# First norms in a row, the first additions of bv put off, an adjacency stage placed under the arrival of Wq, and separate output buffers for the last two batches

## The chip, the cores and the metric

The kernel runs on one core of one Trainium2 chip. The metric is device time in microseconds (us), from start to end of one execution. A profile was taken of one execution of each kernel; its span, from the first to the last instruction, is about 2 us shorter than the device time of the same execution. Where I give a moment without more words, it is counted from the start of that span.

Engine names as in the profile: PE is TensorE (matrix products), PEld its weight loads, DVE is VectorE, ACT is ScalarE, POOL is GpSimd, SP is SyncE. A "q" behind a name is a DMA issue from that engine's queue.

## The reference, cut to what matters

128 batches, each with 128 nodes and 512 features, all float32. Two layers share one adjacency matrix `adj` (128 x 128):

```python
# layer 0
h = maximum(layernorm(x), 0)
A = einsum('od,bdn->bon', adj, h);  C = A + b
x = x + max over j of relu(A[j] + (C - A)[i])      # = relu(max_n A + b): one number c per node
# layer 1: 8 heads of 64
h = maximum(layernorm(x), 0)
q, k, v = h @ Wq + bq, h @ Wk + bk, h @ Wv + bv
w = softmax(q k^T / 8 + (-1e9 where adj == 0))
x = x + w v
```

The second layer norm sees x + c, and c is constant along the features, so it cancels there. The kernel therefore computes h once for each batch, uses it for the adjacency product (whose maximum gives c) and, transposed, for Q, K and V. It adds x, c, bv and the attention's result at the end.

## The kernel before: the parts that the change and the argument touch

Four batches form a group. The first group's Q is computed plainly, everything later with a seven-product scheme. The norm and its end, with the addition of the bias bv on GpSimd:

```python
def norm(m):
    ...
    nc.vector.bn_stats(st, X[g][:, i, :]); nc.vector.bn_aggr(mv, st)
    nc.vector.tensor_scalar_add(ve, mv[:, 1:2], EPS)
    nc.gpsimd.tensor_tensor(rstd, ve, mhalf, op=ALU.pow)          # GpSimd
def norm_end(m):
    nc.vector.tensor_scalar(HN[m], X[g][:, i, :], MV[m][:, 0:1], 0.0, op0=ALU.subtract, op1=ALU.max)
    nc.scalar.activation(HN[m], HN[m], AF.Copy, scale=RSTD[m])
    nc.gpsimd.tensor_tensor(X[g][:, i, :], X[g][:, i, :], bv_sb, op=ALU.add)   # GpSimd, needs bv
def transposes(m):      # 4 PE transposes into one PSUM tile, ACT copies it to HT
def adjacency(m, pa):   # 1 product into PSUM (two matmul records), DVE takes the maximum
```

The beginning (`early(m)` is `transposes(m)` and then `adjacency(m)`), and the first group's K and V:

```python
for m in range(G):                    # G = 4
    norm(m); norm_end(m)
    if m > 0: early(m - 1)
plain_q(0)                            # bias copies on ACT after each half of a PSUM bank
early(G - 1)
weight_sums(nc.vector, "k"); ...h_sum(0, k)...
plain_q(1)
weight_sums(nc.gpsimd, "v")
for s, p in enumerate((k.p1, k.p6, k.p2, ..., v.p4)):   # 13 products
    p()
    m = G + s // 2
    if s % 2 == 0: norm(m); norm_end(m)      # one product ahead of its use
    elif m < 2 * G: early(m)
    else: blocks(m); adjacency(m, ...)
```

The end. `finish` forms w v, divides by the sums, adds x and c, and sends the batch out:

```python
def finish(g, i, w, spare=False, eng=nc.vector):
    ...                                                   # 32 matmuls, reciprocal on DVE
    o = work.tile([P, 2, 4, HD], F32, name="o")           # a pool of two buffers
    nc.vector.tensor_tensor(o, po[...], rs..., op=ALU.mult)
    if eng is nc.vector: eng.scalar_tensor_tensor(y, x_b, c_b, y, op0=ALU.add, op1=ALU.add)
    else: nc.scalar.activation(x_b, x_b, AF.Identity, bias=c_b); eng.tensor_tensor(y, x_b, y, op=ALU.add)
    nc.sync.dma_start(out[b], y)
...
w3 = scores(g, 3, spare=True)
finish(g, 0, w0, eng=nc.gpsimd)
PR[g][2].p3()                                             # V's last product and its addition on DVE
masks(w3)                                                 # two DVE multiplications
finish(g, 1, w1, eng=nc.gpsimd)
finish(g, 2, w2, spare=True, eng=nc.gpsimd)
finish(g, 3, w3)
```

## Time and profile before

The time before is 1616.66 us, the median of four runs (1614.24 to 1617.54); three of them were known when the prediction was made. The profiled span is 1614.1 us. I cut it at five moments. PE's busy time is from the view by windows, at these bounds to 0.1 us.

| Stage of before | from | to | length | PE busy |
|---|---|---|---|---|
| start, until Wq's first product | 0 | 19.80 | 19.80 | 7.54 |
| Q of the first group, until the first K product | 19.80 | 38.32 | 18.52 | 16.24 |
| K and V of the first group, until the first scores | 38.32 | 74.72 | 36.40 | 30.72 |
| main loop, until the last score product | 74.72 | 1598.32 | 1523.60 | 1523.60 |
| end, until the last output sum is done | 1598.32 | 1610.30 | 11.98 | 7.49 |

To read it: in the main loop PE is busy without a gap, so nothing that happens on another engine there matters. In the four other stages PE stands for 12.3, 2.3, 5.7 and 4.5 us. These are the only places where the order of work can win time, some 25 us, and part of that is unavoidable (the first loads, the last output).

### The profile page before, as it was taken

Reading aid. Unit: us, or ns where it says so; the run is one execution under the profiler, and the core shown is the slowest. Engines: PE = TensorE matmul, PEld = TensorE weight load, DVE = VectorE, ACT = ScalarE, POOL = GpSimd, SP = SyncE. Lnnn points to the kernel's source line nnn. Section 1 sums busy time; section 2 is a strip of 40 time slices with the busy share of each in tenths; the row PEclk is TensorE's granted clock in tenths of the full one; section 3 lists DMA queues with packets and bytes.
Section 4 is the critical chain, followed back from the end, with each engine's and each line's share of the span. In section 5 each row is a group of like instructions: output and inputs, shape, how many; then the busy total and the mean of one; then the engine's idle time right before and its main releaser. Section 6 shows DMA issues by size and latency. Waiting matters only on the chain.

```text
span 1614.1 us, 29483 instructions
## 1 busy us (share of the span) xinstructions
PE 1585.8 (98%) x11821; PEld 1318.7 (82%) x11821; DVE 1111.7 (69%) x2044; ACT 425.0 (26%) x847; POOL 263.7 (16%) x281
## 2 busy tenths in 40 slices
PE   6899999999999999999999999999999999999997
PEld 4688888888888888888888888888888888888886
DVE  3576777767777767777667777676776677676655
ACT  2322222222222222222222222222222222222222
POOL 4311111111111111111111111111111111111100
PEclk9999999999999999999999999999999999999999
DMA  4033222232222322222322222322122222223111
GB/s 165 1 73 72 68 56 55 66 79 68 65 45 69 71 73 68 60 50 72 72 69 63 47 69 70 79 63 69 43 70 72 71 68 50 60 69 79 41 30 45
DMA packets 299082, 104.02 MB, mean 64 GB/s; under 512 B 264448, under 2 KB 264576, under 8 KB 298944
## 3 DMA queue, kind: packets, MB, share of 16 engines
q1 hardware_dynamic: 297520, 99.69, 24.5%
q8 instruction: 94, 1.54, 0.4%
q10 hardware_dynamic: 1248, 2.16, 0.4%
q14 instruction: 44, 0.36, 0.1%
q0 software_dynamic: 176, 0.27, 0.1%
HBM read 37.03 MB, written 33.55 MB: 44 GB/s over the span
## 4 chain that ended last, share of the span: by engine, by line
PE 97%; DVE 1%; ACT 1%; POOL 0%; issue 0%; DMA 0%; ACTq 0%; DVEq 0%; POOLq 0%
PE mm L373 72%; PE sc L483 9%; PE pav L511 8%; PE mm L307 6%; PE mm L446 1%; PE pav L307 1%; PE sc L300 0%; POOL rstd L265 0%; DMA xg<-in_x_dram 0%; ACT hn L273 0%; POOL xg L274 0%; DVE st L260 0%; DMA out_dram<-o 0%; ACT qT L451 0%; DVE o L520 0%
## 5 line engine op out<-in xcount | busy, mean ns | idle before, releaser
L265 POOL TENSOR_TENSOR rstd<-ve,mhalf 128x1 f32<-128x1 f32 x128 | 84.5, 660 | 1225.6 <-DVE ve L263 978.5
L494 ACT ACTIVATE w<-sc 128x512 f32<-128x512 f32 x252 | 136.8, 594 | 504.6 <-PE sc L483 504.6
L511 PEld LDWEIGHTS pav<-v,w 128*64 128x64 f32 x4032 | 127.9, 137 | 91.9 <-issue 47.8
L373 PE MATMUL mm<-hs,sq_sb 128*128 128x256 f32 x744 | 179.0, 383 | 0.0
L373 PE MATMUL mm<-sv_sb,hs 128*128 128x256 f32 x768 | 176.6, 379 | 0.0
L373 PE MATMUL mm<-hs,sk_sb 128*128 128x256 f32 x768 | 176.4, 379 | 0.0
L274 POOL TENSOR_TENSOR xg<-xg,bv_sb 128x512 f32<-128x512 f32 x128 | 163.2, 1275 | 34.9 <-DVE hn L270 27.4
L499 DVE TENSOR_TENSOR w<-w,live 128x512 f32<-128x512 f32 x252 | 162.1, 684 | 2.0 <-ACT w L494 2.0
L273 ACT ACTIVATE hn<-hn,rstd 128x512 f32<-128x512 f32 x128 | 92.8, 725 | 267.4 <-DVE hn L270 206.2
L373 PEld LDWEIGHTS mm<-sv_sb,hs 128*128 128x128 f32 x768 | 145.8, 190 | 20.8 <-issue 1.0
L373 PEld LDWEIGHTS mm<-hs,sk_sb 128*128 128x128 f32 x768 | 145.9, 190 | 20.3 <-issue 0.5
L373 PEld LDWEIGHTS mm<-hs,sq_sb 128*128 128x128 f32 x744 | 138.8, 190 | 21.4
L483 PE MATMUL sc<-qT,kT 64*128 64x128 f32 x2048 | 148.7, 285 | 0.0
L511 PE MATMUL pav<-v,w 128*64 128x65 f32 x4032 | 145.3, 224 | 0.0
L483 PEld LDWEIGHTS sc<-qT,kT 64*128 64x128 f32 x2048 | 124.2, 187 | 10.1 <-issue 1.7
L421 DVE TENSOR_TENSOR u<-mm,p1b 128x512 f32<-128x512 f32 x63 | 43.5, 691 | 128.0 <-PE mm L373 128.0
L373 PE MATMUL mm<-hT,wk_sb 128*128 128x256 f32 x512 | 124.2, 385 | 0.0
L373 PE MATMUL mm<-wv_sb,hT 128*128 128x256 f32 x512 | 121.1, 379 | 0.0
L307 PE MATMUL mm<-hn,adjT 128*128 128x512 f32 x236 | 120.5, 592 | 0.0
L373 PE MATMUL mm<-hT,wq_sb 128*128 128x256 f32 x496 | 120.4, 386 | 0.0
L373 PEld LDWEIGHTS mm<-wv_sb,hT 128*128 128x128 f32 x512 | 97.2, 190 | 13.7 <-issue 0.5
L373 PEld LDWEIGHTS mm<-hT,wk_sb 128*128 128x128 f32 x512 | 94.7, 190 | 15.8 <-issue 0.5
(97 smaller groups left out, 2045.5 us busy)
## 6 DMA issues: line engine op xcount, KB each, us to landing
out_dram<-o SPq DMA_DIRECT2D x128, 256.0 KB, 2.1
xg<-in_x_dram SPq DMA_DIRECT2D x62, 512.0 KB, 5.2
hT<-tb SPq DMA_DIRECT2D x960, 32.0 KB, 1.9
xg<-in_x_dram SPq DMA_DIRECT2D x2, 256.0 KB, 3.3
xg<-in_x_dram ACTq DMA_DIRECT2D x2, 256.0 KB, 5.6
wq_sb<-in_L_gnn_Wq_dram SPq DMA_DIRECT2D x1, 512.0 KB, 7.9
wk_sb<-in_L_gnn_Wk_dram SPq DMA_DIRECT2D x1, 512.0 KB, 11.0
wq_sb<-in_L_gnn_Wq_dram ACTq DMA_DIRECT2D x1, 512.0 KB, 11.2
```

What stands on the lines that cost most here:

```text
L265: nc.gpsimd.tensor_tensor(rstd, ve, mhalf, op=ALU.pow)
L273: nc.scalar.activation(HN[m], HN[m], AF.Copy, scale=RSTD[m])
L274: nc.gpsimd.tensor_tensor(X[g][:, i, :], X[g][:, i, :], bv_sb, op=ALU.add)
L307: nc.tensor.matmul(pa, adjT, HN[m], start=True, stop=True)
L373: nc.tensor.matmul(bank[:, r, :], lhs, rhs, start=first and r == 0 and c == 0, stop=r == 1 and c == 1, skip_group_check=True,)
L421: nc.vector.tensor_tensor(self.u3, self.b, self.pf[1], op=ALU.add)
L446: nc.tensor.matmul(bank[:, r, :], W["q"][:, c, k * P : (k + 1) * P], h[:, :, c], start=r == 0 and c == 0, stop=r == 1 and c == NC - 1, ski ...
L483: nc.tensor.matmul(psc[:, j, f, :], KT[g][r, f, i * D : (i + 1) * D], QT[g][r, f, i * D : (i + 1) * D], start=True, stop=True,)
L494: nc.scalar.activation(w[:, j], psc[:, j], AF.Exp, scale=HD ** -0.5)
L499: nc.vector.tensor_tensor(w[:, j], w[:, j], live_h, op=ALU.mult)
L511: nc.tensor.matmul(pav[r, h // 4, (h % 4) * HE : (h % 4 + 1) * HE], w[:, h % 2, h // 2, r], V[g % 2][:, i, h, :], start=True, stop=True,)
```

## The change

Its intent: get PE to Wq's first product earlier, by putting the first four norms in a row and filling the time in which Wq is still travelling with transposes and adjacency products; start each later norm two products ahead of its use; take the bias copies of Q behind a whole bank; move the first four additions of bv, which GpSimd does, into the main loop; and give the last two batches output buffers of their own, so that they don't wait for an output transfer. The diff, cut:

```diff
+        nc.gpsimd.memset(mhalf, -0.5)
+        nc.scalar.activation(live[:, 0:1], mhalf, AF.Copy)      # meant to load ACT's table early
         make_identity(nc, ident)
@@ norm_end
-            nc.gpsimd.tensor_tensor(X[g][:, i, :], X[g][:, i, :], bv_sb, op=ALU.add)
+            if m >= G:
+                add_bv(m)                  # the first four come in the main loop, one a round
@@ transposes, adjacency
-            ph = ps_sc.tile([P, 2, NC, D], F32, name="sc")
+            if i % 2 == 0:
+                PH[g] = ps_sc.tile([P, 2, NC, D], F32, name="sc")
+            ph = PH[g][:, i % 2]           # two batches share a PSUM tile; the same for adjacency
@@ plain_q: bias copies of a bank after both of its halves
@@ finish
-            o = work.tile([P, 2, 4, HD], F32, name="o")
+            if b < B - 2:
+                o = work.tile([P, 2, 4, HD], F32, name="o")
+            else:
+                o = tmp.tile([P, 2, HT2], F32, name="p1b").rearrange(...)
@@ the beginning
             for m in range(G):
                 norm(m)
                 norm_end(m)
-                if m > 0:
-                    early(m - 1)
-            plain_q(0)
-            early(G - 1)
+                if m in (1, 2):
+                    transposes(m - 1)
+            for m in (2, 3):
+                adjacency(m - 2)
+                transposes(m)
+            adjacency(2)
+            plain_q(0, 0)
+            plain_q(0, 1)
+            adjacency(3)
 ... (K's sums, Q's second half, V's sums; norm of batch 4 before Q's last bank)
                 p()
-                m = G + s // 2
-                    if s % 2 == 0:
-                        norm(m); norm_end(m)
-                    elif m < 2 * G:
-                        early(m)
+                if s % 2 == 0 and m < 2 * G + 2:
+                    transposes(m)  (or blocks(m));  adjacency(m);  m += 1
+                    norm(m); norm_end(m)     # now two products ahead of its use
@@ the end
             finish(g, 0, w0, eng=nc.gpsimd)
-            PR[g][2].p3()
             masks(w3)
+            PR[g][2].p3()
```

More of the change, by code (lines that the diff above doesn't have):

```diff
@@ L210, in fast @@
         CNT = []
-        X, HN, TB, HT, HB, QT, KT, C, AMAX, WA, RSTD, MV, PR = ({} for _ in range(13))
+        X, HN, TB, HT, HB, QT, KT, C, AMAX, WA, RSTD, MV, PR, PH, PA = ({} for _ in range(15))
         def load(g):
@@ L236, in fast @@
         load(2)
+        nc.gpsimd.memset(mhalf, -0.5)
+        nc.scalar.activation(live[:, 0:1], mhalf, AF.Copy)
         make_identity(nc, ident)
-        nc.gpsimd.memset(mhalf, -0.5)
         nc.gpsimd.memset(ones, 1.0)
@@ L246, in fast @@
         nc.scalar.copy(adjT, pt[:, :D])
-        nc.vector.tensor_single_scalar(live, adjT, 0.0, op=ALU.not_equal)
         live_h = live.unsqueeze(1).to_broadcast([P, NC, D])
@@ L256, in norm @@
                 C[g] = stat.tile([P, G], F32, name="c")
-            HN[m] = proj.tile([P, N], F32, name="hn")
+            if m in (2, 3):
+                if m == 2:
+                    TB[0] = proj.tile([P, NQ, 2, NC, Q], F32, name="tb")
+                HN[m] = TB[0].rearrange("p a i c r -> p (a i c r)")[:, (m - 2) * N : (m - 1) * N]
+            else:
+                HN[m] = proj.tile([P, N], F32, name="hn")
             st = stat.tile([P, 6], F32, name="st")
@@ L273, in norm_end, with add_bv @@
             nc.scalar.activation(HN[m], HN[m], AF.Copy, scale=RSTD[m])
-            nc.gpsimd.tensor_tensor(X[g][:, i, :], X[g][:, i, :], bv_sb, op=ALU.add)
+            if m >= G:
+                add_bv(m)
+        def add_bv(m):
+            x_m = X[m // G][:, m % G, :]
+            nc.gpsimd.tensor_tensor(x_m, x_m, bv_sb, op=ALU.add)
         def blocks(m):
@@ L297, in transposes, with adjacency @@
             g, i = divmod(m, G)
-            ph = ps_sc.tile([P, 2, NC, D], F32, name="sc")
+            if i % 2 == 0:
+                PH[g] = ps_sc.tile([P, 2, NC, D], F32, name="sc")
+            ph = PH[g][:, i % 2]
             for c in range(NC):
-                nc.tensor.transpose(ph[:, 0, c], HN[m][:, c * P : (c + 1) * P], ident)
-            nc.scalar.copy(HT[g][:, i], ph[:, 0])
-        def adjacency(m, pa=None):
+                nc.tensor.transpose(ph[:, c], HN[m][:, c * P : (c + 1) * P], ident)
+            nc.scalar.copy(HT[g][:, i], ph)
+        def adjacency(m):
             g, i = divmod(m, G)
-            if pa is None:
+            if m >= 2 * G + 2:
                 pa = ps_mm.tile([P, 512], F32, name="mm")
+            else:
+                if i % 2 == 0:
+                    PA[g] = ps_av.tile([P, 2, 512], F32, name="pav")
+                pa = PA[g][:, i % 2]
             nc.tensor.matmul(pa, adjT, HN[m], start=True, stop=True)
@@ L434, in p3, with plain_q @@
                 self.add(self.dst(0, 1), self.c, self.u2)
-        def plain_q(t):
-            if t == 0:
+        def plain_q(t, f):
+            if t == 0 and f == 0:
                 QT[0] = proj.tile([P, NC, T], F32, name="qT")
             h = HT[0][:, 2 * t : 2 * t + 2]
-            for f in range(2):
-                bank = ps_mm.tile([P, 2, HT2], F32, name="mm")
-                for r in range(2):
-                    k = 2 * f + r
-                    for c in range(NC):
-                        nc.tensor.matmul(
-                            bank[:, r, :], W["q"][:, c, k * P : (k + 1) * P], h[:, :, c],
-                            start=r == 0 and c == 0, stop=r == 1 and c == NC - 1,
-                            skip_group_check=True,
-                        )
-                    nc.scalar.activation(
-                        QT[0][:, k, t * HT2 : (t + 1) * HT2], bank[:, r], AF.Identity,
-                        bias=bq_sb[:, k : k + 1],
-                    )
+            bank = ps_mm.tile([P, 2, HT2], F32, name="mm")
+            for r in range(2):
+                for c in range(NC):
+                    nc.tensor.matmul(
+                        bank[:, r, :], W["q"][:, c, (2 * f + r) * P : (2 * f + r + 1) * P],
+                        h[:, :, c], start=r == 0 and c == 0, stop=r == 1 and c == NC - 1,
+                        skip_group_check=True,
+                    )
+            for r in range(2):
+                k = 2 * f + r
+                nc.scalar.activation(
+                    QT[0][:, k, t * HT2 : (t + 1) * HT2], bank[:, r], AF.Identity,
+                    bias=bq_sb[:, k : k + 1],
+                )
         def products(g):
@@ L518, in finish @@
             nc.vector.reciprocal(rs, po[:, :, :, HD])
-            o = work.tile([P, 2, 4, HD], F32, name="o")
+            if b < B - 2:
+                o = work.tile([P, 2, 4, HD], F32, name="o")
+            else:
+                o = tmp.tile([P, 2, HT2], F32, name="p1b").rearrange("p k (h d) -> p k h d", d=HD)
             nc.vector.tensor_tensor(
@@ L543, in fast @@
         with tc.manual_schedule():
-            def early(m):
-                transposes(m)
-                adjacency(m, ps_av.tile([P, 2, 512], F32, name="pav")[:, 0])
             for m in range(G):
@@ L552, in fast @@
                 norm_end(m)
-                if m > 0:
-                    early(m - 1)
-            plain_q(0)
-            early(G - 1)
+                if m in (1, 2):
+                    transposes(m - 1)
+            nc.vector.tensor_single_scalar(live, adjT, 0.0, op=ALU.not_equal)
+            for m in (2, 3):
[5 more added lines that the diff above has]
+            adjacency(3)
             weight_sums(nc.vector, "k")
+            plain_q(1, 0)
+            weight_sums(nc.gpsimd, "v")
             for k in range(4):
                 h_sum(0, k)
-            plain_q(1)
-            weight_sums(nc.gpsimd, "v")
+            norm(G)
+            norm_end(G)
+            plain_q(1, 1)
             _, k, v = PR[0] = [None] + [Products(0, n) for n in "kv"]
+            m = G
             for s, p in enumerate((
@@ L566, in fast @@
                 p()
-                m = G + s // 2
-                if m < 2 * G + 2:
-                    if s % 2 == 0:
+                if s % 2 == 0 and m < 2 * G + 2:
+                    if m < 2 * G:
+                        transposes(m)
+                    else:
+                        blocks(m)
+                    adjacency(m)
+                    m += 1
+                    if m < 2 * G + 2:
                         norm(m)
                         norm_end(m)
-                    elif m < 2 * G:
-                        early(m)
-                    else:
-                        blocks(m)
-                        adjacency(m, ps_av.tile([P, 2, 512], F32, name="pav")[:, 0])
-                if s >= 4 and s % 2 == 0 and s < 12:
-                    weight_sum(nc.gpsimd, "q", s // 2 - 2)
-                if s >= 8 and s < 12:
+                if s in (0, 2, 4, 6):
+                    weight_sum(nc.gpsimd, "q", s // 2)
+                if s in (8, 9, 10, 11):
                     h_sum(1, s - 8)
@@ L589, in fast @@
                 w = scores(g, i)
+                if g == 0:
+                    add_bv(b)
                 for s in range(max(5, len(parts[i]))):
@@ L631, in fast @@
             finish(g, 0, w0, eng=nc.gpsimd)
+            masks(w3)
             PR[g][2].p3()
-            masks(w3)
             finish(g, 1, w1, eng=nc.gpsimd)
```

## The prediction

> **What bounds the kernel now.** I read the page first. TensorE (PE) is busy for 98% of the span and is 97% of the chain that ended last, so only the places where PE is not streaming can be won back.
>
> ```profile
> PE 1585.8 (98%) x11821; PEld 1318.7 (82%) x11821; DVE 1111.7 (69%) x2044; ACT 425.0 (26%) x847; POOL 263.7 (16%) x281
> PE   6899999999999999999999999999999999999997
> PEclk9999999999999999999999999999999999999999
> ```
>
> PE's digit is below 9 only in the first two slices and the last one (40.35 us each). So I read the timeline of the first 76 us and of the last 15 us. From the first score product on, PE never waits until the tail. The beginning:
>
> ```profile
> 7.62 1.11 PE L300 MATMUL sc<-ident,hn 128*128 128x128 f32 x4 [2.31 <-ACT hn L273]
> 8.53 1.91 PE L307 MATMUL pav<-hn,adjT 128*128 128x512 f32 x2
> 10.48 0.69 DVE L308 TENSOR_REDUCE amax<-pav 128x1 f32<-128x512 f32 x1 [2.50 <-PE pav L307]
> 12.10 1.44 DVE L270 TENSOR_SCALAR hn<-xg,mv 128x512 f32<-128x512 f32 x1
> 15.23 1.12 PE L300 MATMUL sc<-ident,hn 128*128 128x128 f32 x4 [4.78 <-ACT hT L301]
> 19.80 1.89 PE L446 MATMUL mm<-hT,wq_sb 128*128 128x256 f32 x8
> 26.54 1.99 PE L446 MATMUL mm<-hT,wq_sb 128*128 128x256 f32 x8 [0.56 <-ACT qT L451]
> 54.00 0.66 PE L300 MATMUL sc<-ident,hn 128*128 128x128 f32 x4 [1.69 <-ACT hn L273]
> 65.66 1.13 PE L307 MATMUL pav<-hn,adjT 128*128 128x512 f32 x2 [1.76 <-ACT hn L273]
> 71.93 1.12 PE L307 MATMUL pav<-hn,adjT 128*128 128x512 f32 x2 [1.69 <-ACT hn L273]
> 74.72 1.16 PE L483 MATMUL sc<-qT,kT 64*128 64x128 f32 x16
> ```
>
> DVE takes batch 0's maximum (10.48) before it begins batch 2's norm. That norm's centring step lasts 1.44 us, against 0.48 elsewhere, while GpSimd adds bv (11.99 to 13.25). ACT is queued behind it, and PE stands 4.78 us. Wq's product starts at 19.80, though Wq's halves landed at 9.6 and 13.4 (issue at 1.67 and 2.17 plus 7.9 and 11.2). Later PE waits for ACT between product halves (0.56 each) and for norms issued too late (1.69, 1.76, 1.69). The end:
>
> ```profile
> 1605.74 0.69 DVE L520 TENSOR_TENSOR o<-sc,RS 128x512 f32<-128x512 f32 x1 [0.37 <-DMA out_dram<-o]
> 1608.82 0.69 DVE L520 TENSOR_TENSOR o<-pav,RS 128x512 f32<-128x512 f32 x1 [2.02 <-DMA out_dram<-o]
> 1609.55 0.75 DVE L526 SCALAR_TENSOR_TENSOR o<-xg,c,o 128x512 f32<-128x512 f32 x1
> ```
>
> The last batch's output buffer is held by an output transfer still in flight.
>
> **What the Trainium skill says.** "DMA: Bandwidth & Descriptors", Anatomy of one DMA: about 2.0 us fixed per transfer, mostly the completion receipt. The trace agrees: outputs land a median 2.1 us after issue, and the last wait is 2.02. "TensorE: Matmul & The Clock Gate", Part 1: PE starts at half clock and gets full clock after about 3.4 us of activity, in a free-running window. The trace agrees in kind: granted clock 0.50 from 15 to 17.5 us, full from about 18; four transposes take 1.11 cold and about 0.5 warm. "ScalarE: Activation LUTs", What ACT_TABLE_LOAD costs: about 1283 ns a load. Here it is 1.28 us, from 5.56. "GPSIMD Engine Reference", Specifications: SBUF interfaces are shared with VectorE, with contention in its two-port mode. The 1.44 us step fits that; I have not tested it.
>
> **The change part by part.**
>
> *Table load early.* A dummy activation now precedes the norms. In the built program it still stands after ACT's own transfer issues, the last of which ran 5.09 to 5.46. The load starts near 5.50 instead of 5.56 and a one-column activation is added: gain about 0. hn of batch 0 ends near 7.65 (7.57 before).
>
> *First norms in a row; bv additions moved.* DVE's norms are 1.4 to 1.5 us each. Batches 0 to 2 run 3.77 to 8.1. Batch 3's x lands near 8.9 (the two loads on ACT's queue have a median of 5.6, and one took 3.9), so its norm ends at 10.4. GpSimd no longer adds bv there; its four additions go to the first four rounds of the main loop, where GpSimd has room (16% busy).
>
> *Transposes in pairs, adjacency behind.* The two halves of a PSUM pair do not free PE as they look: in the built program each transpose still waits for the copy of the one before (same tile), and each adjacency product for the previous maximum. I work it out with cold durations for the first four entries, warm after about 11.1:
> transposes 0: 7.7 to 8.8; copy (0.59) to 9.4;
> transposes 1: 9.45 to 10.55; copy to 11.15;
> adjacency 0: to 11.7; maximum (0.69) to 12.6;
> transposes 2: to 12.1; copy to 12.7;
> adjacency 1: 12.65 to 13.65; transposes 3 in its shadow; maximum to 14.4;
> adjacency 2: 14.4; PE free at 15.2, after Wq's 13.4.
> So Wq's product starts at 15.2 instead of 19.8 with transposes 3 already done: **4.6 us**.
>
> *Q, K, V of the first group.* Eight matmuls of 256 columns go every 1.73 us (starts 81.09 and 82.82), transposes 0.5 a batch (42.48 to 42.97), adjacency 0.86 (42.97 to 43.83). From 15.2:
> Q, 64 matmuls: 64 x 0.2155 = 13.8;
> adjacency 3: 0.86;
> 13 products before the first scores: 13 x 1.73 = 22.5;
> transposes 4 to 7: 2.0;
> adjacency 4 to 9: 6 x 0.86 = 5.2.
> Sum 44.3. Before, 19.80 to 74.72 is 54.9 for 0.5 more work, so 10.1 us are gaps. The new Q halves leave ACT's bias copies behind a whole bank, with another bank open, so the 0.56 waits go. The norm is now issued right behind the previous adjacency product, two K or V products ahead of its use. Its chain (maximum, statistics, rstd on GpSimd, scaling on ACT) took 3.35 us before (43.99 to 47.34), and two products give 3.45: just enough for batches 5 to 7. Batch 8 has 0.2 us more in its chain (the constant c), and batch 9's maximum queues behind a sum and a block transpose: about 0.35 us stall. Batch 4 costs about 0.1. Stalls kept: 0.7. First scores at 15.2 + 44.3 + 0.7 = 60.2 instead of 74.7: **14.5 us in all for the beginning**.
>
> *Main loop.* Same PE work, PE-bound, nothing to win or lose: 0.
>
> *End.* The last two outputs go to the p1b buffers, whose last readers are long done. Masks of the last batch move ahead of V's last addition. I follow the order on DVE: masks to 1602.8, V's sum to 1603.5, output 1 (finish of batch 1) to 1604.4. PE's last product waits for that and runs 1604.6 to 1605.7; reciprocal to 1606.0; last output 1606.0 instead of 1608.82. The final sum ends 1607.45 instead of 1610.30: **2.85 us**. That is a little more than the 0.37 + 2.02 that the waits show, because the reordered masks let output 1 start earlier. GpSimd's output of batch 2 ends near 1606.95, so it does not become the last.
>
> Sum: 14.5 + 2.85 = 17.3. 1616.5 - 17.3 = 1599.2; I say 1599.5 for stalls not foreseen.
>
> **Rivals.**
> (a) The same-tile waits eat the overlap and the clock stays low longer. If transposes do not raise the clock and it comes up only at about 14.5, adjacency 0, 1 and 2 cost some 1.4 us more in series: 1601. For it: the second batch of before was cold again. Against: PE now works nearly without pause from 7.7.
> (b) The norm chain, with 0.1 us of slack, becomes the bound of the K and V stage: with 0.5 us lost on each of five batches, 2.5 us back: 1602. For it: three waits of 1.7 in the same place now, and ACT carries the bias copies in the same queue. Against: the norm starts two products ahead.
> (c) Wq or its siblings are later: DMA runs at its peak (about 390 GB/s) till 20 us. The start cannot go below 13.4 in any case; two more microseconds there would give 1601.
> (d) The end is bound elsewhere (the last transfer's 2 us, GpSimd's two outputs): only 1 us gained there, 1601.
> (e) Better than thought: all stalls vanish and the clock warms early: 1597.5.
>
> **Range and chances.** The changes touch 76 us at one end and 10 at the other; everything else is fixed by PE. Even a perfect beginning and end could not make the 32 us for 2%, and a loss of 2% would need stalls in the steady loop, for which I see no cause. The runs of before spread 2.6 us. Range 1596.5 to 1603.
>
> **What would show it.** First scores (L483's successor) near 60 us; the first Wq product near 15; the copies and maxima of the first four batches each followed by a PE start within 0.1 us, which shows the same-tile waits; no PE wait above 0.5 us between 20 us and the first scores; DVE's centring step of batch 2 at 0.48; the table load still near 5.5. At the end, DVE's output products without a DMA wait and the final sum about 3 us earlier against the span's end. I am wrong if the main loop's length moves by more than 1 us, or the beginning gains under 11 or over 17.

## The result, and the profile after

The changed kernel takes **1601.87 us**, the median of four runs (1601.37 to 1602.05), against 1616.66 for the kernel before in the same rounds. The ratio is 0.991, with a 95% interval of 0.9893 to 0.9928. A ratio here is the mean time of one kernel's fast runs over that of the other's fast runs of the same rounds, so it is not quite the ratio of the medians. All runs were fast (none more than 1.5% above the fastest of its kernel), at a mean granted clock, the share of its full speed that PE was given, of 0.999 in the changed kernel. All outputs are right. The 14.8 us are real: the two sets of four runs lie over 12 us apart.

First two lines from the page of the changed kernel, busy time of each engine and PE's tenths in 40 slices of the span:

```profile
PE 1584.6 (99%) x11821; PEld 1319.4 (82%) x11821; DVE 1112.2 (70%) x2044; ACT 424.5 (27%) x848; POOL 264.0 (17%) x281
...
PE   7999999999999999999999999999999999999998
```

PE's busy time fell by only 1.2 us, while the span fell by 14.3. So what went was waiting, not work. Both digits that had been low in front (6 and 8) rose, and the last one went from 7 to 8.

Next the view by windows of the changed kernel, cut at its own five moments (Wq's first product at 16.45, first K product at 31.12, first scores at 61.80, last score product at 1585.40, end of the last output sum at 1595.93). The columns are: window, its length, busy time of each engine with instructions in brackets, granted clock of PE, DMA share, GB/s.

```profile
core 0: us, PE busy (x) PEld busy (x) DVE busy (x) ACT busy (x) POOL busy (x), PEclk, DMA share, GB/s
0.00:16.40 16.40, 8.19 (x23) 4.53 (x24) 7.04 (x19) 6.56 (x11) 6.60 (x18) 1.00 0.85 289
16.40:31.10 14.70, 14.70 (x67) 12.54 (x66) 7.24 (x13) 2.52 (x6) 4.98 (x4) 1.00 0.35 129
31.10:61.80 30.70, 30.51 (x134) 22.93 (x132) 21.02 (x44) 10.50 (x20) 18.17 (x17) 1.00 0.00 1
61.80:1585.40 1523.60, 1523.60 (x11446) 1272.85 (x11445) 1067.42 (x1951) 402.03 (x806) 230.11 (x239) 1.00 0.26 63
1585.40:1596.00 10.60, 7.46 (x155) 6.50 (x154) 9.10 (x16) 2.91 (x5) 4.13 (x3) 1.00 0.14 52
```

| Stage | before | after | difference | predicted |
|---|---|---|---|---|
| start, until Wq's first product | 19.80 | 16.45 | -3.35 | -4.6 |
| Q, then K and V, until the first scores | 54.92 | 45.35 | -9.57 | -9.9 |
| main loop | 1523.60 | 1523.60 | 0.00 | 0 |
| end | 11.98 | 10.53 | -1.45 | -2.85 |
| sum | | | -14.37 | -17.3 |

The Q, K and V stages are now full: PE is busy for 14.70 of 14.70 and for 30.51 of 30.70 us. The main loop did not change by 0.01 us, and in all runs below it is 1523.59 to 1523.61 us, so every difference between kernels lies in the start or the end. (Q's stage alone fell by 3.85 us, more than the 2.3 that PE stood there: 0.5 us of its work, batch 3's transposes, now lies in the start, and the rest had been counted as busy, since the profile models where a matmul ends.) What is left to explain is the start and the end.

The beginning of the changed kernel, from its timeline. The columns are start, busy time, engine, line, operation, output<-input, size and number of instructions, and in brackets how long the engine stood idle before and what released it:

```profile
5.50 1.28 ACT L239 ACT_TABLE_LOAD   x1 [5.50 <-DMA xg<-in_x_dram]
...
7.59 0.48 DVE L275 TENSOR_SCALAR tb<-xg,mv 128x512 f32<-128x512 f32 x1
...
7.66 1.11 PE L312 MATMUL sc<-ident,hn 128*128 128x128 f32 x4 [2.36 <-ACT hn L278]
...
9.45 1.12 PE L312 MATMUL sc<-ident,hn 128*128 128x128 f32 x4 [0.68 <-ACT hT L313]
...
10.36 1.92 PE L323 MATMUL pav<-hn,adjT 128*128 128x512 f32 x2
...
12.07 1.06 PE L312 MATMUL sc<-ident,tb 128*128 128x128 f32 x4
...
13.06 1.64 PE L323 MATMUL pav<-hn,adjT 128*128 128x512 f32 x2
...
14.54 0.60 PE L312 MATMUL sc<-ident,tb 128*128 128x128 f32 x4
...
15.48 1.13 PE L323 MATMUL pav<-tb,adjT 128*128 128x512 f32 x2 [0.34 <-DVE amax L324]
...
16.45 7.07 PE L460 MATMUL mm<-hT,wq_sb 128*128 128x256 f32 x32
...
52.82 1.12 PE L323 MATMUL pav<-hn,adjT 128*128 128x512 f32 x2 [0.15 <-ACT hn L278]
...
61.80 1.16 PE L499 MATMUL sc<-qT,kT 64*128 64x128 f32 x16
```

The reader is to see three things. Batch 2's centring step (7.59) is back at 0.48 us. Between 7.66 and 16.45 PE goes from one entry to the next, but the entries are slow: the first adjacency product takes 1.92 us and the second 1.64, batch 2's transposes 1.06; only from 14.54 are they fast (0.60). And the one wait that is left in the K and V stage worth naming is 0.15 us, at 52.82.

The end:

```profile
1588.54 2.37 DVE L515 TENSOR_TENSOR tb<-tb,live 128x512 f32<-128x512 f32 x2
1588.76 1.60 POOL L548 TENSOR_TENSOR o<-xg,o 128x512 f32<-128x512 f32 x1 [80.05 <-DVE o L539]
...
1590.83 0.68 DVE L410 TENSOR_TENSOR v<-mm,u 128x512 f32<-128x512 f32 x1
...
1593.92 1.26 POOL L548 TENSOR_TENSOR p1b<-xg,p1b 128x512 f32<-128x512 f32 x1 [0.17 <-DVE p1b L539]
1594.02 0.69 DVE L539 TENSOR_TENSOR p1b<-pav,RS 128x512 f32<-128x512 f32 x1
...
1595.18 0.75 DVE L545 SCALAR_TENSOR_TENSOR p1b<-xg,c,p1b 128x512 f32<-128x512 f32 x1 [0.47 <-POOL p1b L548]
```

The DMA waits of 0.37 and 2.02 us before the output products are gone. In their place are two things that the prediction does not have: the two masks of the last batch take 2.37 us (1.28 before, in the line below), and the last sum stands 0.47 us.

```profile
1603.13 1.28 DVE L499 TENSOR_TENSOR tb<-tb,live 128x512 f32<-128x512 f32 x2
```

### The profile page after: what moved, and what is told of

Same layout as the page of the kernel before. It is cut to its first block, busy times and chain, and to the rows that moved or that the text cites. A ratio compares the mean times of both kernels' runs of the same rounds, so it can differ in the third digit from the quotient of the medians.

```text
span 1599.8 us, 29471 instructions
## 1 busy us (share of the span) xinstructions
PE 1584.6 (99%) x11821; PEld 1319.4 (82%) x11821; DVE 1112.2 (70%) x2044; ACT 424.5 (27%) x848; POOL 264.0 (17%) x281
## 4 chain that ended last, share of the span: by engine, by line
PE 99%; DVE 1%; DMA 0%; ACT 0%; POOL 0%; issue 0%; POOLq 0%; ACTq 0%
PE mm L389 73%; PE sc L499 9%; PE pav L527 8%; PE mm L323 6%; PE mm L460 1%; PE pav L323 1%; PE sc L312 0%; DMA xg<-in_x_dram 0%; DVE tb L515 0%; DVE st L265 0%; DVE amax L324 0%; ACT hn L278 0%; POOL p1b L548 0%; PE sc L527 0%; DVE hn L275 0%
```

## The experiments

Three questions: which part of the change gave what; what had made PE stand before Wq's product in the kernel before; and why start and end each gained about 1.3 us less than predicted. I name an experiment by what it does. Where there is one time only, its granted clock (0.998 or 0.999) is given by the trace, and I compare moments within the traces.

Moments vary too. Six traces have the changed kernel's beginning as it stands (its own and those of the runs with the old end, the late norms, the half-bank copies, the masks put back, and the PSUM operands at the end). In them Wq's product starts between 16.04 and 16.92, so a smaller difference than 0.88 us there shows nothing. In all six it starts 1.75 us after the end of the second adjacency product. That product's own time, 1.15 to 2.02 us, makes nearly all of the spread.

### The two parts alone

The changed kernel with the old end, and the old kernel with the new end:

```diff
 (changed kernel, old end)
-            if b < B - 2:
-                o = work.tile([P, 2, 4, HD], F32, name="o")
-            else:
-                o = tmp.tile([P, 2, HT2], F32, name="p1b").rearrange(...)
+            o = work.tile([P, 2, 4, HD], F32, name="o")
...
-            masks(w3)
             PR[g][2].p3()
+            masks(w3)
```

> The changed kernel with the end of the kernel before (output buffers of the work pool, last masks after V's last addition). If beginning and end are independent, the first score product stands at 61.8 us as in the changed kernel, the last output sum ends 11.98 us after the start of the last score product as in the kernel before, and the span is 1599.8 + 1.45 = 1601.2 us. If the two parts interact (the main loop takes another rhythm), the stretch from first to last score product differs from 1523.6 by more than 0.5.

> The kernel before with the new end alone. Independent parts: last output sum ends 10.5 us after the start of the last score product, span 1614.1 - 1.45 = 1612.7. If the end gives the 2.85 us that I predicted and something of the new beginning takes half of it back, 9.1 us and a span of 1611.3.

Measured: the beginning alone takes 1603.51 us (1603.27 to 1603.76), ratio 0.9917 (0.9901 to 0.9934); the end alone 1615.62 us (1614.69 to 1615.83), ratio 0.999 (0.9974 to 1.0007), both against a median before of 1616.88 in the same rounds. That is 13.4 and 1.3 us, in sum 14.6, against 14.8 for the whole change. The parts add up, so the end's lost microsecond is not something that the beginning took away. With the old end, the last output product waits 2.39 us for an output transfer and the last sum ends 12.36 us after the last score product starts. So the buffers do what they were made for. The end-alone result by itself is not distinguishable from no change by its interval; the trace, with 10.33 us for the end, is what shows it. Its span was 1614.0 and not the expected 1612.7, because the unchanged old beginning was slower in this execution: Wq's product starts at 21.29 and the first scores at 76.20, against 19.80 and 74.72.

### Only the additions of bv moved

The kernel before, with nothing but the four first bv additions moved to the main loop. The order of rows on DVE, which the prediction had blamed, stays as it was.

```diff
-            nc.gpsimd.tensor_tensor(X[g][:, i, :], X[g][:, i, :], bv_sb, op=ALU.add)
+            if m >= G:
+                add_bv(m)
...
                 w = scores(g, i)
+                if g == 0:
+                    add_bv(b)
```

> The kernel before with one part of the change alone: the bv additions of the first four batches moved into the main loop. Theory A: in the kernel before, batch 1's rstd stood in GpSimd's queue behind batch 0's bv addition, which waited for bv to land at 11.9 us, and that was the hole before 15.2; then without it batch 1's rstd runs near 6.4, batch 1's transposes near 10.4 and Wq's first product near 16 instead of 19.8, first scores near 71. Theory B, the one of my prediction: DVE's order (maximum of batch 0 before the norm of batch 2) made the hole; then Wq's first product stays within 1 us of 19.8.

Why I suspected it: GpSimd's timeline of the kernel before.

```profile
3.50 0.56 POOL L234 DMA_DIRECT2D bv_sb<-in_L_gnn_bv_dram  x1
...
5.03 0.67 POOL L265 TENSOR_TENSOR rstd<-ve,mhalf 128x1 f32<-128x1 f32 x1 [0.24 <-DVE ve L263]
11.99 1.26 POOL L274 TENSOR_TENSOR xg<-xg,bv_sb 128x512 f32<-128x512 f32 x1 [6.30 <-DVE mv L261]
13.21 0.74 POOL L265 TENSOR_TENSOR rstd<-ve,mhalf 128x1 f32<-128x1 f32 x1
```

GpSimd computes rstd of batch 0 at 5.03 and then stands for 6.30 us in front of batch 0's bv addition. Bv was issued at 3.50 and needs 8.4 us from issue to landing (the view of DMA issues), so it lands at 11.9. The bracket names a DVE instruction as the releaser, but that one had long been done. Rstd of batch 1 is queued behind this addition, runs at 13.21, and ACT's scaling of batch 1 and PE's second transposes (15.23) follow from it.

Measured: 1611.69 us (one run), and in its timeline Wq's product starts at 15.60, which is 4.2 us earlier than in the profiled execution before (and 5.7 earlier than in the end-alone run, which has the old beginning too):

```profile
10.47 0.69 DVE L313 TENSOR_REDUCE amax<-pav 128x1 f32<-128x512 f32 x1 [2.50 <-PE pav L312]
11.08 0.68 DVE L260 BATCH_NORM_STATS2 st<-xg 128x6 f32<-128x512 f32 x1
...
15.60 1.89 PE L451 MATMUL mm<-hT,wq_sb 128*128 128x256 f32 x8
```

DVE still takes batch 0's maximum ahead of batch 2's norm, as the lines show, and the hole is gone all the same. So the wait for bv in GpSimd's queue made it. Norms in a row and the new order of transposes and adjacency products bring Wq's start no further, as far as single traces can tell: the full change starts it at 16.45, 0.85 us later than this one line of change, but with batch 3's transposes already done, which cost PE about 0.5 us later on.

### The norms one product ahead again

The changed kernel, with the norms in the K and V stage back where they were before.

```diff
-                if s % 2 == 0 and m < 2 * G + 2:
-                    transposes(m) (or blocks(m)); adjacency(m); m += 1
-                    norm(m); norm_end(m)
+                if s % 2 == 0: norm(m); norm_end(m)
+                else: transposes(m) (or blocks(m)); adjacency(m)
```

> The changed kernel with the norms of batches 4 to 9 issued where the kernel before has them, one product ahead of their use instead of two. Theory: from the first K product to the first scores the kernel before took 36.4 us and the changed one 30.7; so this one takes about 36.4, first scores near 67.5, span near 1605.5, with waits of 1 to 2 us for the scaled norm again. Rival: the 5.7 us came from the order of GpSimd's weight sums or the pairing of PSUM tiles, which stay here; then the stretch stays near 30.7.

Measured: 1607.16 us, 5.3 us above the changed kernel's median. From the first K product to the first scores it takes 36.18 us against 30.68; before it was 36.40. The earlier norms give nearly all of what the K and V stage gained.

### Bias copies after each half of a bank

```diff
-            for r in range(2):          # the bias copies moved back into the loop of products
                 k = 2 * f + r
                 nc.scalar.activation(QT[0][:, k, ...], bank[:, r], AF.Identity, bias=bq_sb[:, k : k + 1])
```

> The changed kernel with the bias copies of the first Q again behind each half bank, as in the kernel before. Theory: four waits of PE for ACT come back, 0.56 us as shown plus the restart, so from the first Wq product to the first K product 14.7 + 2.3 to 3.3 = 17 to 18 us, first scores near 64.5. Rival: the kernel before lost that time to its interposed transposes and adjacency product; then the stretch stays within 0.5 of 14.7.

Measured: 1609.09 us; Q's stage takes 21.95 us instead of 14.67, so it loses 7.3 us, more than twice what was expected. The 0.56 us waits are back, and there is one large wait besides, in the timeline of this run:

```profile
35.26 3.50 PE L460 MATMUL mm<-hT,wq_sb 128*128 128x256 f32 x8 [3.02 <-ACT qT L466]
```

In the changed kernel the norm of batch 4 is issued before Q's last bank. ACT's queue then holds batch 4's scaling between the two halves' copies: ACT stands 3.09 us for that batch's rstd, and PE stands behind ACT. After that wait the granted clock is 0.50 (35 to 36 us), and the eight products shown take 3.50 us instead of 1.89; so some 1.6 of the 7.3 us are the clock. So the two edits belong together: an earlier norm without the later copies would have been a loss here.

### Own PSUM tiles for the first four batches

The prediction had said that the two halves of a PSUM pair don't free PE, because each entry still waits for the reader of the one before in the same tile.

```diff
+            if m < G:
+                ph = ps_mm.tile([P, 512], F32, name="mm").rearrange("p (c d) -> p c d", d=D)
...
+            elif m < G and i % 2 == 1:
+                pa = ps_sc.tile([P, 2, NC, D], F32, name="sc")...[:, 0]
+            elif m < G:
+                pa = ps_av.tile([P, 2, 512], F32, name="pav")[:, 0]
```

> The changed kernel with a PSUM tile of its own for each of the first four transposes and adjacency products. Theory: the same-tile waits hold PE between 8.8 and 16.4; without them batch 1's transposes start right behind batch 0's near 8.8 (9.45 now), and Wq's first product starts near 15.2 instead of 16.45. Rival: the low clock and the late x of batch 3 (10.25) fill that stretch anyway; then Wq's first product stays within 0.3 of 16.45.

Measured: 1600.37 us; Wq's product starts at 14.45, 2.0 us earlier than in the changed kernel. Transposes 0 and 1 now run together, in 1.97 us from 7.71, and adjacency products no longer wait for the maximum before. 0.5 us of it is lost again later, as PE waits 0.56 us for batch 4's scaling at 31.57. In this run batch 3's x landed at 9.0 instead of 10.25, and the second adjacency product, at 12.03, was already mostly warm (1.28 us); so not all of the 2.0 us, more than the expectation, need come from the tiles. That the waits on a shared tile were real is shown by transposes 0 and 1 running together.

### A warm clock

Six dummy products of the identity with itself, while nothing else is ready for PE.

```diff
+        wu = ps_av.tile([P, 2, 512], F32, name="pav")
+        for k in range(6):
+            nc.tensor.matmul(wu[:, 0, 0:P], ident, ident, start=True, stop=True)
```

> The changed kernel with six extra products of the identity with itself, unused, between adj's transpose (4.8 us) and batch 0's transposes (7.7), so that PE is active 3 us earlier. My prediction took the clock as full from about 11.1; the changed kernel showed cold durations until about 14 (batch 2's transposes 1.06, adjacency 0 1.92, adjacency 1 1.64). Theory: the cold clock is what put Wq's first product 1.25 us after my 15.2; with an earlier start of activity adjacency 0 takes about 1.0 to 1.5 us, batch 2's transposes 0.6, and Wq's first product starts near 15. Rival: the chain of copies and maxima and batch 3's late x set it; then it stays within 0.3 of 16.45. The phase of the clock's window may spoil this look.

Measured: 1600.28 us. The dummies ran from 5.09, Wq's product starts at 14.87 instead of 16.45, and the first adjacency product takes 1.02 us instead of 1.92, as this run's timeline has it:

```profile
9.80 1.02 PE L326 MATMUL pav<-hn,adjT 128*128 128x512 f32 x2
```

So the clock accounts for about 1.6 us of the start. The Trainium skill, "TensorE: Matmul & The Clock Gate", Part 4: PE-mode transpose, says that transposes do not count as PE-busy in the same way for the clock. The trace of the changed kernel agrees: PE transposed from 7.66 on, yet the adjacency products at 10.36 and 13.06 were still slow, and all was fast from 14.54. No run tests this apart from how busy PE was. When the clock rises isn't fixed either. In the six traces with one and the same beginning, the second adjacency product starts 2.7 us after the first in each, and takes anything from 1.15 us (nearly warm) to 2.02 (cold). The last two experiments below share a beginning with dummies from 5.10: in one the first adjacency product takes 1.59 us at 9.37, in the other 1.02 at 8.70.

### The table load earlier

The dummy activation moved between ACT's own transfer issues, ahead of K's half.

```diff
+        nc.gpsimd.memset(mhalf, -0.5)
         for name, src in (("q", wq), ("k", wk), ("v", wv)):
+            if name == "k":
+                nc.scalar.activation(live[:, 0:1], mhalf, AF.Copy)
```

> The changed kernel with the dummy activation ahead of ACT's last two transfer issues instead of behind them, and the constant it reads set first on GpSimd. Theory: in the changed kernel the table load starts at 5.50 because ACT's queue issues transfers until 5.46, so the part of the change gained nothing; here it starts near 3 and ends near 4.3, batch 0's scaling starts when its rstd is there (5.7 instead of 6.90), its transposes near 6.5 instead of 7.66, and Wq's first product 0.5 to 1.2 us earlier than 16.45. Rival: the later issue of the second halves of Wk and Wv, or batch 3's x, takes it back: Wq's first product within 0.3 of 16.45.

Measured: 1600.6 us. The load starts at 2.68 instead of 5.50, batch 0's first transposes at 6.61 instead of 7.66, and Wq's product at 15.15, 1.3 us earlier. 0.82 us of that is there when the second adjacency product starts (12.24 instead of 13.06); the other 0.48 is its shorter time (1.16 instead of 1.64), which varies as much on the same code. The changed kernel has the right idea, but places the dummy behind the issues.

### The masks put back behind V's last product

```diff
-            masks(w3)
             PR[g][2].p3()
+            masks(w3)
```

> The changed kernel with the last masks again after V's last addition; the output buffers stay new. Theory: moved forward, the masks run beside GpSimd's first output sum, both read two operands from SBUF, and the pair took 2.37 us instead of 1.28 and GpSimd 1.60 instead of 1.27; put back, they take 1.28 and GpSimd 1.27, and the last output sum ends within 0.4 us of the 10.53 after the last score product's start (what the masks gain V's addition order loses). Rival: the reordering is worth the 0.46 us that my prediction gave it; then 11.0 or more.

Measured: 1602.41 us; the last sum ends 10.44 us after the last score product begins, against 10.53. The masks take 1.28 us again and GpSimd's first output sum 1.27. The changed kernel's end took 10.53 or 10.54 us in five traces and 10.33 and 10.32 in two others, so the 0.09 is no gain of either order. Moving the masks ahead was worth nothing.

### One operand of the masks, and the last result, in PSUM

```diff
+            lp = ps_mm.tile([P, 512], F32, name="mm"); nc.scalar.copy(lp[:, :D], live)
-            masks(w3)
+            masks(w3, lp[:, :D]...)               # the mask is read from PSUM
...
+            if b == B - 1:
+                op = ps_mm.tile([P, 512], F32, name="mm")   # last quotient in PSUM
```

> The changed kernel with the live mask for the last batch read from PSUM and the last normalised output kept in PSUM, so that DVE's last masks and last sum read only one operand from SBUF. Theory (two SBUF operands on DVE wait for GpSimd's instruction): the masks take 1.28 us beside GpSimd, V's last addition comes 1.1 us earlier, the last sum doesn't wait 0.47 for GpSimd, and it ends near 9.1 us after the last score product's start, span near 1598.4. Rival (the stretch is a semaphore wait or general slowness of SBUF): masks stay at 2.4 and the end stays at 10.5.

Measured: 1600.75 us. The end takes 9.73 us. The masks are still ahead and still beside GpSimd's sum, but nothing slows them, by the timeline of this run:

```profile
1588.13 1.27 DVE L515 TENSOR_TENSOR tb<-tb,mm 128x512 f32<-128x512 f32 x2
1588.34 1.28 POOL L557 TENSOR_TENSOR o<-xg,o 128x512 f32<-128x512 f32 x1 [80.04 <-DVE o L550]
```

The Trainium skill, "SBUF — State Buffer", Who interferes with whom, says that a DVE instruction with two SBUF inputs contends with a GpSimd instruction that reads SBUF, and that the one that starts first holds the shared ports for its whole instruction while the other blocks. The changed kernel's trace agrees to within 0.15 us. Taken singly, its two masks last 0.68 and 1.77 us. GpSimd starts inside the first and is 0.33 us longer than its usual 1.27; the second mask ends 0.55 us after GpSimd does (1590.91 and 1590.36). With one input in PSUM both last as long as alone. The 0.47 us before the last sum, however, stayed.

### All of it together

Own tiles, dummy products, early table load, the mask in PSUM and the last quotient in PSUM, and the order of the beginning adapted (transposes 3 inside Q's first half, K's weight sums and the sums of hT before adjacency 3, the norm of batch 4 earlier). C is added to x on ACT, so that the last sum has one SBUF input and one in PSUM.

> All that the runs so far showed, together: own PSUM tiles for the first four batches, early table load, warm-up products, the third batch's transposes behind the first half of Q, K's weight sums and the sums of hT before adjacency 3 on DVE, mask of the last batch from PSUM, and the last output sum as a plain sum of x (c added on ACT) and a PSUM tile. Theory: Wq's second half lands at 13.6, so its product starts at 13.7 to 14.3; first K product near 29, first scores near 59.6 (61.8 in the changed kernel), last output sum ends near 9.1 after the last score product (10.53), span near 1596.2, time near 1598.3. If the last sum's wait for GpSimd came from the form with a pointer operand rather than from two SBUF tensors (it stayed 0.47 with one), it is gone now; if it stays, it is neither.

Measured: **1597.34 us** (1596.95 to 1597.49), ratio to the kernel before 0.9882 (0.9865 to 0.9898), so it is faster than both kernels. Wq's product starts at 12.96, 0.3 us before Wq's second half lands (13.3); its first products read only the first half, and PE shows no wait. So the start has nearly come to the transfer. The end takes 9.68 us, with the same 0.47 us before the last sum, although it no longer has two SBUF inputs.

### The sum before the last one on DVE

One more try at the 0.47: GpSimd is given nothing to do while the last sum is due.

```diff
-            finish(g, 2, w2, spare=True, eng=nc.gpsimd)
+            finish(g, 2, w2, spare=True)
```

> The combined version, with the output sum of the last batch but one on VectorE instead of GpSimd, so that GpSimd has nothing to do while the last sum is due. So far the last sum stood 0.47 us in every kernel with the new beginning, in the combined version too (0.47 after the product into PSUM), and it began each time about 0.1 us after GpSimd's sum of the batch before had ended. Theory A: GpSimd's sum holds it. Then the wait is at most 0.1 us here; the sum of the batch before costs VectorE about 0.75 us, which delays the reciprocal by about 0.45 us, so the last sum ends about as long after the start of the last score product as before, 9.7 us (9.5 to 9.9), and the whole stays at 1597.3. Rival B: the wait belongs to the last sum or to what it reads, whatever GpSimd does. Then it stays near 0.47 us, the last sum ends at about 10.2 us after that start, and the whole is about 1597.8.

Measured: 1597.19 us (1597.17 to 1597.74), ratio 0.988 (0.9864 to 0.9897). The last sum, from the two timelines, first with GpSimd busy in the combined version and then here:

```profile
1591.09 0.69 DVE L559 TENSOR_TENSOR p1b<-xg,mm 128x512 f32<-128x512 f32 x1 [0.47 <-DVE mm L555]
```

```profile
1590.77 0.69 DVE L559 TENSOR_TENSOR p1b<-xg,mm 128x512 f32<-128x512 f32 x1
```

The wait is gone: the same instruction starts 0.1 us after the product's end (1590.67). It goes with GpSimd's sum of the batch before. DVE now carries 0.79 us more itself, so the end takes 9.83 us and the whole gains nothing that could be told from noise (in the profiled executions its beginning, the same code, reached the first scores 0.47 us earlier). What does the holding is not settled. The shared ports fit the changed kernel, where the last sum starts at 1595.18, exactly when GpSimd's sum ends. They do not fit the combined version, where the last sum reads one operand from PSUM and yet starts only 0.13 us after GpSimd's end. Nor is the form always the same: in the end-alone run and in the one with the late norms, both with the changed kernel's end, the last sum began 0.1 us after the product, but took 0.92 and 0.91 us, and ended 0.55 and 0.54 us after GpSimd's sum. And with DVE's order also changed here, GpSimd's idleness is the likeliest, not the only, difference.

## Why the prediction was right or wrong, point by point

**The time.** 1601.87 lies 2.4 us above the predicted 1599.5, inside the range of 1596.5 to 1603, and the gain stayed under the 2% that it ruled out. The sum of the stages was predicted as 17.3 us and came out as 14.4.

**What bounds the kernel: right.** Only PE's gaps could be won back. The main loop's 1523.60 us in both kernels confirm the predicted 0.

**The cause of the hole before Wq's product: wrong.** The step that failed is "DVE takes batch 0's maximum before it begins batch 2's norm" and what was hung on it. The bv experiment kept that order and won 4.2 us. The hole was rstd of batch 1 behind the bv addition in GpSimd's queue, which waited for bv until 11.9. The reading went wrong because it asked what PE, ACT and DVE did and never listed GpSimd's own timeline; the DVE centring of 1.44 us was a side effect of the same late addition: with the addition moved it took 0.48 us at the same place (12.09). It had run from 12.10 to 13.54 and GpSimd's addition from 11.99 to 13.25; that it ended 0.29 us after the addition fits its being blocked, which no run tests. That the predicted size came near the truth was luck in this: the change happens to move the bv additions too, so the predicted order of work could come about.

**The size of the start, 4.6 us: too much by 1.25.** The failed step is "warm after about 11.1". It was worked out from PE's first transposes at 7.7, which did not warm the clock. Rival (a), full clock only at about 14.5 and 1.4 us lost in series, is what happened: the first two adjacency products and batch 2's transposes took 1.92, 1.64 and 1.06 us instead of the 1.02, 1.12 and 0.63 that the dummy products made of them. That experiment got about 1.6 us back. Batch 3's x landed at 10.25 instead of the estimated 8.9, and that cost nothing: in the six traces with this beginning it landed between 8.72 and 10.25, and Wq's product always started 1.75 us after the end of the second adjacency product.

**The waits on a shared tile: right**, and worth up to 2.0 us at Wq's start when removed. **The table load's gain of 0: right**, 5.50 against 5.56; moved truly ahead it was worth 0.8 to 1.3.

**Q, K and V: right.** From Wq's product to the first scores it took 45.35 us against the predicted 45.0. The parts hold too: undoing the early norms gives 5.5 us back, undoing the late bias copies 7.3. The second shows an interaction that the prediction's separate terms didn't contain.

**The end, 2.85 us: too much by 1.40.** The mechanism, the wait for the output transfer, was right: the 2.02 and 0.37 us are gone. The failed step is "masks to 1602.8, V's sum to 1603.5, output 1 ... to 1604.4". It gave the masks 1.3 us in their new place, without asking what ran beside them. In the trace they end 5.51 us after the last score product begins instead of 4.48, which arrives as 0.94 us at the last output product. The rest is the 0.47 us wait of the last sum. The promised extra from the reordering (0.46 us) was nothing: with the masks put back the end was 10.44 us against 10.53. A contention rule was quoted in the prediction, but for the start, and not applied to the order that the change makes at the end. One of the signs named, the final sum 3 us earlier "against the span's end", can't be read as worded, since that distance was 3.8 us before and 3.9 after.

**Rivals.** (b), a norm chain without slack, fell: the largest wait left in the K and V stage is 0.15 us. (c), a late Wq, fell: PE was later than Wq. (d), only about 1 us at the end, came close in size, but by contention and not by the transfer or GpSimd's outputs becoming the last. (e) fell.

## What to carry to other kernels

When an engine stands, list the queue of every engine in the chain in order, above all that of the one which does only small things: an instruction that waits for a late load holds all that is queued behind it, and a releaser that the profile names but that had long been done is the hint. When a change moves instructions, look at what will run beside them in the new place; a DVE instruction with two SBUF inputs and a GpSimd instruction that reads SBUF took turns here, so 1.28 us of work took 2.37. At a cold start, products of dummy data while PE has nothing to do, an activation ahead of the last transfer issues, and own PSUM tiles each took 1.3 to 1.6 us off the device time in single runs, and 4.5 together with the mended end. Before such differences are read, look at how much the same code varies from trace to trace: here Wq's start varied by 0.88 us.

## What the Trainium skill lacked or had wrong

- "TensorE: Matmul & The Clock Gate" has the warm-up, says that transposes don't count (which these traces support), and warns that clock events in a trace can be unreliable. How far, it leaves out: here the view by windows gives a granted clock of 1.00 for 0 to 16.4 us, while the adjacency product took 1.92 us against 1.02 warm. Durations decide.
- "ScalarE: Activation LUTs", What ACT_TABLE_LOAD costs, adds 1380 ns of drain to 1283 ns of load, for every switch to a different set. Here the load took 1.28 us and the next activation began at 6.79, 0.01 us after it; no drain shows at this first load.
- None of the pages I read says that an early dummy activation loads the table early only if it stands ahead of the transfer issues in ACT's queue: here the load started at 5.50 us behind them and at 2.68 between them.
- "SBUF — State Buffer" and "GPSIMD Engine Reference" have the rule of two SBUF inputs, and the masks follow it (2.37 us against 1.27 with one input in PSUM). It does not cover the last sum, which waited 0.47 us beside GpSimd's sum with one SBUF input too, and 0.1 when GpSimd was idle. What holds it is open.
